# Weight sums of two slots in one operation, in place, and six plain slots instead of seven

## The chip, the cores and the metric

The kernel runs on one core of a Trainium2 chip. The metric is the device time of one execution in microseconds (us). Three runs of the kernel before took 715.67, 717.20 and 717.89 us; the median is 717.2 us. All times below come from those runs or from one profiled execution on the hardware.

## What is computed

For each of four batches of 1024 tokens with 512 features the reference does

```python
scale = cond @ norm_w.T + 1.0
ms = jnp.mean(x * x, axis=-1, keepdims=True)
h = x * (scale[:, None, :] * jax.lax.rsqrt(ms + EPS))
u = h @ up_w.T                       # up_w: 4096 x 512
val, gate = jnp.split(u, 2, axis=-1)
h = val * jax.nn.gelu(gate, approximate=False)
hq = h + jax.lax.stop_gradient(act_quant(h) - h)
wq = down_w + jax.lax.stop_gradient(weight_quant(down_w) - down_w)
y = hq @ wq.T                        # down_w: 512 x 2048
return y + x
```

`act_quant` rounds every row to 8-bit integers by its largest value, `weight_quant` rounds the weights to -1, 0 and 1.

## The kernel before

**Tiling.** The 2048 channels of the hidden layer are 16 slots of 128 (`j` = 0 to 15), each with a value half and a gate half of `up_w`: two 128 x 512 blocks, 512 KB together. A batch's tokens are two halves of 512. A matmul here has a 128 x 128 stationary block and 512 columns, and every f32 operand is split into a high and a low f16 part, so that one product of two blocks takes three f16 matmuls.

**Two kinds of slots.** A plain slot (`plain_half`, lines 803-834, and `plain_first` for slot 0) does value and gate for two token halves straight: 4 results x 12 = 48 matmuls. The other slots (`slot`, lines 858 on) take the value and gate block as a 2 x 2 scheme of seven products in place of eight, each with six matmuls of 512 columns: 42 matmuls. For the seven products the four quarter blocks of a weight slot must first be added and subtracted: `s_sums`, lines 523-529, four operations of 128 x 256 on f32. In the first batch the weights are being built, and slots `j < SEVEN` = 7 are plain, the nine others go by the seven products; in the three later batches all slots do, from what the first batch prepared.

**Steps for a slot's weights** in the first batch: SP loads them (`w_load`) into a buffer of `H` that `W_SLOT` names; their largest value gives a power of two (`w_range`, line 447 a DVE reduction), POOL or ACT multiplies by it (`w_scale`, lines 474-476); `w_rows` splits them into f16 parts (ACT line 499, DVE line 500) in the buffer `H[:, 15 + j % 2]` and issues a transposing transfer (line 501). `s_sums` writes the four combinations to one shared buffer `sf` = `H[:, 17]`. `s_high` (ACT, line 539) and `s_low` (line 543, DVE for odd slots, POOL for even ones) split these; `s_spill` writes the slot to DRAM, with a transposing transfer ahead for slots of the seven products (line 554 and 547). Later batches load it back (`s_load`).

**What sets the order.** All engines' instructions are first recorded by the code (class `Book`), and then emitted in an order that is written out as a packed table `ORDER`. Each engine runs its own queue in that order, with semaphores between the engines. So the program order of the code says what depends on what, and the table says what stands ahead of what on an engine.

**The start.** PE begins with matmuls on zeros (`keep_warm`, line 1185), then transposes the first tokens (line 1169) and the weights of slots 0 and 1 (line 484), whose f16 parts ACT and DVE write out (lines 509 to 521 for weights, 1173 and 1177 for tokens), and starts with slot 0 (line 849). The tokens of the second half (tiles 4 to 7) are scaled by 1/rms on ACT and POOL (lines 1162 and 1164) and transposed a little later.

Of the kernel before, what the change touches and what calls it, by code (L numbers as in the profile page):

```python
# [13 lines left out]
F16 = mybir.dt.float16  # L14
# [9 lines left out]
P = 128  # L24
# [12 lines left out]
PLACE = {4: 0, 5: 1, 6: 2, 2: 3, 3: 4, 0: 5, 1: 6}  # L37
# [35 lines left out]
class Book:  # L73
# [29 lines left out]
    'c-mcB2Y40b5}i#j1V|{UKnOh`AWcA2qzQsb5wU><MHEGv=(8fI=tD(CY@nz#dj~A2s7O&kB%vcBAU&az0MfGa&YAz;oA~zol6&vo',  # L103
    '-M`G7Idf+A#!DsnM^9)C*`bx>u%6Phq`Dl@Ku+s16{#k>HAxcXfTl~nhFS&Jq)T*^l@rQ8kt(tZW9;?c)sX`IORGsaDaP1)HAfEV',
    'Z(3REW41MVj#R)k+jR%t9oNm;1fP#;MOh`aFw#D)D?jN4_$EmL`AgHJBK|)o4{A1MN|ZPWb#&bL;&j=iTQR~(O_iVZLitnAmNU9b',
    '<D{od)C$r<j$v-@W4$()PV$3}kpbEocNJsC19}jjpVBiJbq7|yQw#Mn*`!4nvyaThnS3oL9c8k%kYVzgay7}=MI3fi9u^xUZ`#g_',
    'Gz0TA#5V!fbp$r-CLifVvKVt$k}}vq7Iu0Bdq0G|<>2!lN(&`PBRLDUEwWF;<tx2Zrfa6G*E+Z|Q@+rivJAUujBoSwJ$**H$_Shj',
    '`3@^7(gsqfH6>M+W8Ru_P4H~U`5WSFh&^u8suB-tEWkQn!ajK1CU59KsU=fz)nP3o_2h3|jFtX_I}X5x4ROab{ahv~eKtwjVr4f<',
    '6P&#l?=F^0qzzV(fsu-&hu$q$;4Bd%u+)CNL%xCKI8PRA`K)fl4tirQfnTn{4vu3LPvUivc9!>Wwk@ukti2=~))CpFyRp*sc7Kk1',
    'ua{t#T<<MF#uCldmB2)j+%8kGFCsDrqw>l|*z+K)Bn@krXzTnA_wsmJ9?%~0rS=Qn5Bd41{w^JKr?vvND@rq<HNtQ@P&){#_}0$U',  # L110
    '2X-C_{;_)|N<H8zMHXp$e3~NH!&^P&79EORUo5}l`d8&Hl|aKHtqt6+z?l|7UYIV;v5xMr2uJB83xMWdl&}1&2n1HZtSR_zqcl*i',
    ';CEp6sHR)|?6terNGoMrr2wh*Y@I!2pmxCLclCOF`pcgci=;$&&mAlDT+G-T{#gsZo@3|Q%agW)TGB@U126un^ifq<w!O5I&-8Y9',
    'U4ZqUFyC+5M$SiEFEAfv0v+Fg2g(E0uVTg&87H$eA9!}N(HC{#y-~25$Z<njBlxk0EJbuQm#VTyS7|ex&6fGVYzBDYGrbbH-LG8f',
    '^Lh`ydrt2~RJ4`Ru<mM20spka+PcC=1sJsr)<jlF!@7R8dC!9dGhnkCwuTS&S{qm71HBHPc~v#U#5Vm0c6k;%K82Yd1?~h9w+2!F',
# [12 lines left out]
    '`N0kP4$gFzHQ_nIOdTNgbrU{MN8C4;l^TYhY2Sd^hdUw4sOcQ<Qioh9V*K)ju@FaI0&d@L`R#W@ri=EDng=eb<aUM(5UruE#d0}Z',
    'odJul#{WbptqiH7TZrmY^UgY>%pmQ(u5fV>WfFeQ56cAH)5C~Y&ag=n;7uMIfzcw*W<0h*K?$<cUoi!+0`D4G_9n0Gv)6V&KN0WL',
    '`Dv`>05atVSm_tg2#vvDE{l?tm_z^8TKMCg35ahhx&qUE9N{=n&MZ+8df;yR*7+<2ag*%r=u{!E+O4bww&>e>BSyRk49}7F0eu-B',
    '6O6Zb=nZ!`Pw<ab0{`|P$IJ<@!19ZsB*@$!A=edRuIL~_ocF#$Y*Sem=^lL_t7A5-59@6}G{W*wgQ*h5cf5QjotgKgFIcRMIP5(o',  # L130
    'S85(+`6s3i$miX`r*C1EJQ6LwmV$SYk>pZbmx|RaKwO<4yW<3EizpWp2P5=F8Hg<2-(q1Nl>TDFQCH-_ESVuU+m+K0#R9~<1@%-0',
    'vB=|h=+#kBwhm>qhf_M640n&pW2Pt>8$)z5xIGUZ%rh$$K<l=YXY_vQ4IWr;@myetEKsti$dAyhwZU`Ff=}s#(B=K{_bs%?-?9C_',
    'j~q$0SVl4|KgA<+5Q{bCaUE+&p}z-#VVLioU3g@I^%C*Q6}W@ku}i55oK-l+7-ZX~h8A~@>Z+q$q>Js2_fU;)(s8EsiOn1JZJga~',
    '*vSV6bKN40@C3_4laY}&Tjuys%A0<<2i&m4W)z%Bv6{1nc`+Mn5!fLcx`j2b)0JBh4|_c}({!I<s;y~oSLI%%pWs|Ya96y|AlUhv',
    'R>QD@;&BVCM=ob(ZKHq3Fi{S;?IErbOVT3dMDT|@nC(yLquBdOb$fL7K{cWEf_NyotNoR$p_-{SE{Db>4q1J3ohLoh6A3pU%WO49',
    'As<yUPNClx7I%mnswZ`-uu7#`A~M{H#a2e;OLV%*KH2!<Pg8f?(fRtT<xR2tahq;IMMaGF(CL~MxcZhereYPFQCIW6>%d@{xZB0e',
    'UU2SqWxnOeWbbMc)jI;6BEgGFl`%|TwljA@0iQsmufeDfLko<uv*V!P>tRO$Y(!MwtTRf26|2}{48j;lg&mTly6%c`lvqYz3>*E8',
    'wO6%@;FM--uCRJYK%Q-`D{W20Rx9~jnR$<BCbGEG8dMb`pB0~qyB6O~^=o%p#OeCW5#i0`-$y55ymfX_jI8A97U&Mt$?nLq%vQtf',
    'JqDOBqo*CdphHU6dVfIut_UBHm+TWON~*`_w6i7$vu!n%v7@72tv_BeE4X7NkiE>VA)-%UC9V9Z7h?BUffKhN7Yp)ITiE4YX#2}h',
    'nTXXwEB#K%NUUZr!25T=mS2WFf?P0-$me10pt(>3P1Av>zMqb*d8@tvHWrIx@^N&2Ay&8mZ0?xyb+AWH@PIO=u0XYW7>ewDWMi_;',  # L140
    'WBRBucX>T#9%LTm@es5IH9uJ)#g9r>BtP7Q$e0W4T_>NYtGoE^D5&z0c%7yDeZ;bwz8~MQR^FubOL>h-IqGO_!4=dY(Rb~GMd1kS',
    '`(~)hRr(0@HL`~uM(rV{!N$XfPSO9P>~_%}D}kS{f%#W-s8zj}Ayd2l0KK->bf&A8uLXlO^qrzYSYbUp>5d`LF$JDesa+nijzPp1',
    'B8?@r)D8~X$cOxQ<ShYbzid@;U;Py4Ccu85V(x-4!%#_n-W^s8rs-PbiRc(73&J(v$N!jC?x&Ag)%iB!<^}!JFj!4@%N?j29B*cT',
    'C$nUt)e+B!_XKxB`HQsGb$YWYu^!MSB?oh5GhO9BO_4j1DJtkuDXDsMq3xdmQc`_4U>U~E)hA&0`lyXXt^vD>SFyC`o5%_qG1t;?',
    'Sn!*khMscDkjS5;S8KVzRUn@L^@(yTSSnu`%cJE<oAEWd1Fx^+-S=S^v&(JBbfYa(eS#b^QeH$&Xk8ib^~Zjdw_s=PT`%CGuW7S4',
    '^frsAD}kUSi;kmUC}xcYhGKRivSXI`0H3ZkW^l&<RAp1)9oDq0hXqyRD7jB3m?Btc)jT7cSRQNjm%DGX*7e<nlZcC3EIW(UMekYW',
    '<iY&C7HTfZXJ(fpj~U}RmEts2itqE1wW}E`eI4Y4nO;e;Q$r<R!LHundotU!sn^Er!>|*{Dt|Y)>qsoui>cU%|EZkQe8qFdYpva;',
    'CJv(xt`$>yJAKs<)j6zWb4;(z2yPB*!lG2>3&CGU5E)rQ6qiIbwex;W@ShkN8Mt$u@nK0na6j~E`o9>LkysK9n@!_)g)%%0{H#NC',
    'Ugf{}P|1|_y*A)%)E0keO<ff<3xV`NVzr%L5n`<ncjSA!?6xlaB57~9*sdLepTaa#KO&8S^&$V(hE0O9(jxdhj58~U=WW*mAxpg!',
    '4iD&+BI}`t>hkt8P@H7yWUrr@?|-&>=b*2q#VcE<H{;=(Jl{`^EM5lpRx;l@%&>FA>$f7l`iUE%x>d*Z@Q!PsnrBy_53;HFxaUY`',  # L150
# [1602 lines left out]
```

## Time and profile before

| what | value |
|---|---|
| three runs | 715.67, 717.20, 717.89 us |
| the profiled execution's own time | 716.0 us |
| its span, first to last instruction | 714.2 us |
| granted TensorE clock, mean | 1.000 |
| busy: DVE, ACT, POOL | 527.8, 432.8, 144.2 us |
| read from and written to DRAM | 63.73 and 23.11 MB |

PE is TensorE, DVE VectorE, ACT ScalarE, POOL GpSimd, SP the engine that issues the transfers. A group line gives the source line, the engine, what is written and read (partitions x elements), how often, the busy time and the mean duration in ns, then the idle time just ahead of it and who ended it. A line of windows gives start and end, then the busy time of PE, PE's weight loads, DVE, ACT and POOL with the number of instructions in brackets, the granted clock, the DMA engines' busy share and GB/s. A line of the timeline gives start and duration in us, engine, line and operation. Durations there include the fill of a pipelined engine, so neighbours on PE and DVE overlap by a little.

### The profile page before, as it was taken

What the parts mean: (1) busy time and instruction counts of PE and PEld (TensorE: products, weight loads), DVE (VectorE), ACT (ScalarE), POOL (GpSimd) and SP (SyncE); (2) the same over time, 40 slices, a digit from 0 to 9 for tenths busy, and PEclk for the clock granted to TensorE, in tenths of its full rate; (3) what the DMA queues carried; (4) which work ended last, traced back from release to release, by engine and by line L of the source; (5) the groups of instructions that cost most, each with busy time, mean ns of one, the idle gap of its engine ahead of it and who ended that gap; (6) DMA issues with size and microseconds to landing.
All of it is one profiled execution on the core that took longest, in us unless ns stands there. A gap on an engine that the chain in (4) does not pass through costs nothing.

```text
span 714.2 us, 10170 instructions
## 1 busy us (share of the span) xinstructions
PE 707.6 (99%) x3642; PEld 357.5 (50%) x3642; DVE 527.8 (74%) x837; ACT 432.8 (61%) x739; POOL 144.2 (20%) x161
## 2 busy tenths in 40 slices
PE   8999999999999999999999999999999999999998
PEld 4544444444444446655444455555444444444854
DVE  7968899998478896767659756775638846547895
ACT  5688889886578675654547476453434565334362
POOL 3675521120200005440202032800110000000010
PEclk9999999999999999999999999999999999999999
DMA  8778999999899973777345754566344354433324
GB/s 291 237 223 221 232 230 275 230 190 228 260 212 238 248 238 92 231 165 152 99 133 121 153 142 123 155 171 120 72 137 159 82 132 98 110 118 111 120 87 165
DMA packets 182943, 121.46 MB, mean 170 GB/s; under 512 B 144598, under 2 KB 150503, under 8 KB 182892
## 3 DMA queue, kind: packets, MB, share of 16 engines
q1 hardware_dynamic: 182346, 120.68, 64.8%
q8 instruction: 28, 0.46, 0.2%
q14 instruction: 23, 0.19, 0.1%
q10 hardware_dynamic: 546, 0.13, 0.1%
HBM read 63.73 MB, written 23.11 MB: 122 GB/s over the span
## 4 chain that ended last, share of the span: by engine, by line
PE 98%; DVE 2%; issue 0%
PE A L791 41%; PE E L791 21%; PE B L791 10%; PE po L1077 9%; PE E L806 5%; PE A L806 3%; PE B L806 2%; PE po L1027 2%; PE E L1027 1%; PE B L1077 1%; PE A L1027 1%; PE A L1185 1%; DVE wam L447 0%; PE E L1077 0%; PE A L1077 0%; PE B L1027 0%
## 5 line engine op out<-in xcount | busy, mean ns | idle before, releaser
L791 PEld LDWEIGHTS <-SXY 128*128 128x128 f16 x2226 | 217.7, 98 | 247.7 <-issue 0.2
L791 PE MATMUL A<-R,SXY 128*128 128x512 f16 x1200 | 291.0, 379 | 0.0
L791 PE MATMUL E<-R,SXY 128*128 128x512 f16 x600 | 152.5, 379 | 0.0
L923 ACT ACTIVATE gm<-H 128x512 f32<-128x512 f32 x120 | 75.6, 630 | 56.0 <-DVE R L924 45.3
L924 DVE TENSOR_TENSOR R<-R,gm 128x512 f32<-128x512 f32 x120 | 85.7, 714 | 29.1 <-ACT gm L923 28.5
L868 DVE TENSOR_TENSOR E<-A,v 128x512 f32<-128x512 f32 x57 | 39.7, 697 | 60.6 <-PE A L791 51.6
L791 PE MATMUL B<-R,SXY 128*128 128x512 f16 x318 | 82.7, 379 | 0.0
L1004 DVE TENSOR_TENSOR H<-H,am 128x1024 int8<-128x1024 f32 x64 | 77.0, 1222 | 0.0
L1009 ACT CAST R<-H 128x1024 bf16<-128x1024 int8 x64 | 65.3, 1042 | 18.1 <-DVE H L1004 17.9
L942 POOL PARTITION_ALL_REDUCE am<-R x8 | 15.6, 1950 | 256.8 <-DVE R L924 256.8
L1077 PE MATMUL po<-wd,R 128*128 128x256 fp8e4 x448 | 63.2, 273 | 0.0
L885 ACT ACTIVATE t<-B,sg 128x512 f32<-128x512 f32 x57 | 38.9, 682 | 36.2 <-PE B L791 36.1
L876 ACT COPY B<-A 128x512 f32<-128x512 f32 x57 | 32.8, 576 | 44.5 <-PE A L791 37.8
L1077 PEld LDWEIGHTS <-R 128*128 128x128 bf16 (+1 forms) x512 | 50.1, 98 | 18.7
L888 DVE SCALAR_TENSOR_TENSOR H<-A,sg,t 128x512 f32<-128x512 f32 x57 | 42.5, 746 | 20.7 <-PE A L791 19.8
L904 DVE TENSOR_TENSOR v<-A,v 128x512 f32<-128x512 f32 x57 | 39.1, 686 | 22.1 <-PE A L791 21.8
L901 ACT ACTIVATE t<-E,sg 128x512 f32<-128x512 f32 x57 | 38.7, 681 | 24.4 <-PE E L791 24.4
L907 DVE SCALAR_TENSOR_TENSOR H<-v,sg,t 128x512 f32<-128x512 f32 x57 | 45.2, 794 | 8.1 <-ACT t L901 8.0
L880 ACT COPY v<-E 128x512 f32<-128x512 f32 x57 | 33.2, 582 | 19.9 <-PE E L791 12.8
L806 PEld LDWEIGHTS <-SXY 128*128 128x128 f16 x216 | 21.0, 98 | 24.7 <-issue 0.3
L655 POOL TENSOR_SCALAR ssq<-ssq 128x2 f32<-128x2 f32 x12 | 4.2, 349 | 143.0 <-ACT xt L684 109.2
L1118 DVE SCALAR_TENSOR_TENSOR xr<-po,dq,xr 128x256 f32<-128x256 f32 (+1 forms) x36 | 21.8, 608 | 9.9 <-PE po L1077 4.4
(286 smaller groups left out, 864.1 us busy)
## 6 DMA issues: line engine op xcount, KB each, us to landing
SXY<-s_dram SPq DMA_DIRECT2D x63, 256.0 KB, 3.3
SXY<-s_dram SPq DMA_DIRECT2D x21, 384.0 KB, 3.4
H<-in_L_cond_up_w_dram SPq DMA_DIRECT2D x13, 512.0 KB, 4.8
s_dram<-SXY SPq DMA_DIRECT2D x6, 896.0 KB, 5.7
xr<-in_x_dram SPq DMA_DIRECT2D x19, 256.0 KB, 3.8
out_dram<-xr SPq DMA_DIRECT2D x19, 256.0 KB, 3.2
H<-in_x_dram SPq DMA_DIRECT2D x8, 512.0 KB, 5.1
s_dram<-SXY SPq DMA_DIRECT2D x10, 384.0 KB, 5.1
```

What stands on the lines that cost most here:

```text
L791: PE.matmul(o, s[:, w, k, :], xs(l, k), start=start and n == 0, stop=stop and n == len(TERMS) - 1, skip_group_check=True,)
L806: PE.matmul(ps, a[k // 2][:, w, k % 2, :], XP[:, l, k, h * TOK : (h + 1) * TOK], start=n == 0, stop=n == len(terms) - 1,)
L868: DVE.tensor_tensor(cur["E"], cur["A"], cur["v"], ALU.add)
L885: ACT.activation(cur["t1"], pb, AF.Gelu, scale=gain(g, 1))
L888: DVE.scalar_tensor_tensor(h_half(g - 1, 0), prev["A"], gain(g - 1, 0), prev["t1"], ALU.mult, ALU.mult)
L904: DVE.tensor_tensor(cur["v"], cur["A"], cur["v"], ALU.add)
L907: DVE.scalar_tensor_tensor(h_half(g - 1, 1), prev["v"], gain(g - 1, 0), prev["t2"], ALU.mult, ALU.mult)
L923: ACT.activation(gm, v, AF.Abs)
L924: DVE.tensor_tensor(m, m, gm, ALU.max)
L1004: DVE.tensor_tensor(whole(v), v, r.to_broadcast([P, 2, TOK]), ALU.mult)
L1009: ACT.copy(q, by_tile(whole(v)))
L1077: PE.matmul(po, w[:, j], m, start=start and j == 0, stop=stop and j == n - 1, skip_group_check=True,)
```

## The change

Five things are changed in the code. The four sums of a slot are now made for two slots at once: the operations are 128 x 2 x 256, and `s_sums` is called for even `j` only. They are written back over the slot's own weight blocks, so `sf` becomes a view of the slot's weight buffer, and `W_SLOT` puts slots `j` and `j + 1` of a pair side by side. Because the weights are overwritten, the f16 rows for the transposing transfer are split off earlier, by a function of its own (`w_cast`), in `H[:, 16 + j % 2]`. `SEVEN` is 6, so slot 6 goes by the seven products. Two buffers are moved (`FT`, the junk output of `first_sum(0)`), and the table `ORDER` is replaced as a whole.

```diff
-PLACE = {4: 0, 5: 1, 6: 2, 2: 3, 3: 4, 0: 5, 1: 6}
+PLACE = {6: 0, 4: 1, 5: 2, 2: 3, 3: 4, 0: 5, 1: 6}
...
 ORDER = (
-    '5*6$@hON`O)6`g^sV=9S)9n`y1+l00@~>`h$?-py<lOQ',
...
-    W_SLOT = [14, 12, 13, 8, 9, 10, 14, 12, 13] + 3 * [14, 12, 13]
+    W_SLOT = [14, 15, 12, 13, 8, 9, 10, 11] + 2 * [12, 13, 14, 15]
...
-    sf = H[:, 17].rearrange("p t (n f) -> p (t n) f", n=2)
+    def sf(j):
+        return wn(j).rearrange("p t (n f) -> p (t n) f", n=2)
...
-    SEVEN = 7
+    SEVEN = 6
...
+    cast = set()
+
+    def w_cast(j):
+
+        cast.add(j)
+        n = H[:, 16 + j % 2].bitcast(F16).rearrange("p t (n w f) -> p (t n) w f", n=2, w=2)
+        a = 0 if j < SEVEN else 1
+        ACT.copy(n[:, a:, 0], sf(j)[:, a:])
+        DVE.tensor_tensor(n[:, a:, 1], sf(j)[:, a:], n[:, a:, 0], ALU.subtract)
+
     def w_rows(j):
 
-        v = H[:, 15 + j % 2].bitcast(F16).rearrange("p t d -> p (t d)")
-        n = v.rearrange("p (n w f) -> p n w f", n=4, w=2)
-        f = wn(j).rearrange("p t (n f) -> p (t n) f", n=2)
+        if j not in cast:
+            w_cast(j)
+        v = H[:, 16 + j % 2].bitcast(F16).rearrange("p t d -> p (t d)")
         a = 0 if j < SEVEN else 1
-        ACT.copy(n[:, a:, 0], f[:, a:])
-        DVE.tensor_tensor(n[:, a:, 1], f[:, a:], n[:, a:, 0], ALU.subtract)
...
     def s_sums(j):
-        v = wn(j).rearrange("p t (n f) -> p t n f", n=2)
-        a11, a12, a21, a22 = v[:, 1, 0], v[:, 1, 1], v[:, 0, 0], v[:, 0, 1]
-        (POOL if j < 4 else DVE).tensor_tensor(sf[:, 0], a21, a22, ALU.add)
-        (POOL if j < 4 else DVE).tensor_tensor(sf[:, 2], a11, a21, ALU.subtract)
-        (POOL if j < 6 else DVE).tensor_tensor(sf[:, 1], sf[:, 0], a11, ALU.subtract)
-        (POOL if j < 6 else DVE).tensor_tensor(sf[:, 3], a12, sf[:, 1], ALU.subtract)
+
+        c = W_SLOT[j]
+        v = H[:, c : c + 2].rearrange("p s t (n f) -> p s t n f", n=2)
+        a11, a12, a21, a22 = v[:, :, 1, 0], v[:, :, 1, 1], v[:, :, 0, 0], v[:, :, 0, 1]
+        eng = POOL if j < 4 else DVE
+        eng.tensor_tensor(a22, a21, a22, ALU.add)
+        eng.tensor_tensor(a21, a11, a21, ALU.subtract)
+        eng.tensor_tensor(a11, a22, a11, ALU.subtract)
+        eng.tensor_tensor(a12, a12, a11, ALU.subtract)
...
-    FT.append(H[:, 11])
+    FT.append(H[:, 7])
...
         if n == 0:
-            j = wn(0)[:, 0]
+            j = H[:, 0, 0]
...
-        if n < NJ:
-            s_sums(n)
...
-        if n < NJ:
-            s_all(n)
         if j + 3 < NJ:
             w_scale(j + 3)
             if j < SEVEN:
                 w_rows(j + 3)
+            elif j % 2 == 0:
+                w_cast(j + 3)
+        if j % 2 == 0 and n < NJ:
+            s_sums(n)
+        if n < NJ:
+            s_all(n)
```

The new table moves instructions on every engine. Three places follow. The source lines of the kernel after are some 8 to 11 higher from line 500 on.

The first is DVE at the start, just ahead of PE's first matmul of slot 0. `E_103` and `po_102` are PSUM buffers that hold transposed weights and tokens; line 509 (517 after) writes weights, line 518 (526 after) their low part, line 1177 (1188 after) the low part of tokens, line 1145 (1156 after) sums a token tile's squares. Before:

```order
L447 TENSOR_REDUCE wam_99<-H 128x2
L454 TENSOR_SCALAR sw<-wam_104 128x2
L321 TENSOR_SCALAR wam_99<-wam_99 128x2
L457 RECIPROCAL iv_106<-sw 128x2
L454 TENSOR_SCALAR sw<-wam_99 128x2
L509 CAST SXY<-E_103 128x2x256
L457 RECIPROCAL iv_105<-sw 128x2
L518 TENSOR_TENSOR SXY<-E_103,SXY 128x2x256
L1177 SCALAR_TENSOR_TENSOR R<-po_101,scT,R 128x512
```

The same place on DVE after the change:

```order
L447 TENSOR_REDUCE wam_99<-H 128x2
L320 TENSOR_SCALAR wam_104<-wam_104 128x2
L320 TENSOR_SCALAR wam_99<-wam_99 128x2
L454 TENSOR_SCALAR sw<-wam_104 128x2
L454 TENSOR_SCALAR sw<-wam_99 128x2
L457 RECIPROCAL iv_106<-sw 128x2
L457 RECIPROCAL iv_105<-sw 128x2
L1156 SCALAR_TENSOR_TENSOR R,ssq_0_88<-H 128x512
L1188 SCALAR_TENSOR_TENSOR R<-po_102,scT,R 128x512
L517 CAST SXY<-E_103 128x2x256
```

The sum of squares and a low part of tokens have moved ahead of the first cast of weights; the low part of weights, which stood directly behind the cast, comes later.

The second is PE at the same time: its step into slot 0. `E_98`, `A_91`, `po_102` are PSUM buffers, the rows of line 1185 (1196 after) the matmuls on zeros. Before:

```order
L484 MATMUL E_98<-ident,H 128x128
L1169 MATMUL po_102<-ident,H 128x128 x2
L1169 MATMUL A_91<-ident,H 128x128
L1185 LDWEIGHTS H
L1185 MATMUL A_94<-H 128x512
L849 LDWEIGHTS SXY
L849 MATMUL B_92<-R,SXY 128x512
```

After the change PE has this order there (line 860 is line 849 of before):

```order
L1196 MATMUL A_94<-H 128x512
L484 MATMUL E_103<-ident,H 128x128
L484 MATMUL po_102<-ident,H 128x128
L860 LDWEIGHTS SXY
L860 MATMUL A_94<-R,SXY 128x512
L484 MATMUL po_102<-ident,H 128x128
L1180 MATMUL A_91<-ident,H 128x128
L484 MATMUL po_102<-ident,H 128x128 x2
```

Slot 0 now begins with its value half (buffer `A_94`) rather than its gate half (`B_92`), and behind transposes of slot 1's weights into `po_102`, the buffer that DVE's line 1188 reads before.

The third is POOL from slot 0's sums on: lines 526 to 529 are the four sums, 476 scales weights, 656 (667 after) computes 1/rms of token tiles 4 to 7, and 1164 (1175 after) scales tiles 5 and 7 by it. Before:

```order
L529 TENSOR_TENSOR H<-H 128x256
L656 TENSOR_TENSOR rs_0_89<-ssq_0_88,neghalf 128x4
L543 TENSOR_TENSOR SXY<-H,SXY 128x3x256
L1164 TENSOR_SCALAR H<-H,rs_0_89 128x512 x2
L526 TENSOR_TENSOR H<-H 128x256
```

The same stretch on POOL after, from the first sum of slots 0 and 1 (line 537) on:

```order
L537 TENSOR_TENSOR H<-H 128x2x256
L476 TENSOR_SCALAR H<-H,iv_106 128x512
L667 TENSOR_TENSOR rs_0_89<-ssq_0_88,neghalf 128x4
L538 TENSOR_TENSOR H<-H 128x2x256
L1175 TENSOR_SCALAR H<-H,rs_0_89 128x512
L454 TENSOR_SCALAR sw<-wam_99 128x2
L539 TENSOR_TENSOR H<-H 128x2x256
L476 TENSOR_SCALAR H<-H,iv_100 128x512 x2
L1175 TENSOR_SCALAR H<-H,rs_0_89 128x512
```

Tile 7's scaling, which stood directly behind tile 5's, now has a sum of two slots and two weight scalings ahead of it; slot 0's low part (line 543), which stood ahead of both, has gone behind.

170 lines of the change are left out of this document (84 added, 86 removed).

## The prediction

> **What bounds the kernel now.** I read first the page's line of busy times and the chain of work that ended last.
>
> ```profile
> PE 707.6 (99%) x3642; PEld 357.5 (50%) x3642; DVE 527.8 (74%) x837; ACT 432.8 (61%) x739; POOL 144.2 (20%) x161
> PE 98%; DVE 2%; issue 0%
> ```
>
> PE is busy for 99% of the span and is 98% of the chain. A busy PE need not be at its pitch, so next the timeline of PE in the first batch, at products of six matmuls of 512 columns:
>
> ```profile
> 163.59 1.46 PE L791 MATMUL A<-R,SXY 128*128 128x512 f16 x6
> 164.88 1.46 PE L791 MATMUL A<-wd,R 128*128 128x512 f16 x6
> 166.18 1.46 PE L791 MATMUL E<-wd,SXY 128*128 128x512 f16 x6
> ```
>
> Starts are 1.295 us apart for six, so one costs 0.216 us. Then the windows of the first batch, where the changed work lies (PE, PE's weight loads, DVE, ACT, POOL, then clock, DMA share, GB/s):
>
> ```profile
> 0.00:20.00 20.00, 16.76 (x85) 9.33 (x86) 16.00 (x71) 11.17 (x22) 7.31 (x14) 1.00 0.89 299
> 20.00:40.00 20.00, 20.00 (x103) 10.24 (x101) 17.26 (x32) 14.01 (x29) 15.51 (x21) 1.00 0.74 226
> 80.00:100.00 20.00, 20.00 (x95) 9.06 (x93) 19.89 (x35) 17.91 (x33) 4.83 (x5) 1.00 0.93 251
> 140.00:160.00 20.00, 20.00 (x95) 9.08 (x93) 18.63 (x32) 16.29 (x30) 5.34 (x7) 1.00 1.12 219
> ```
>
> All PE idleness that an order could remove lies before 20 us; behind it PE is full. DVE is full from 80 to 100 us (19.89 of 20) and yet makes PE wait nowhere. So the time can fall in two ways only, fewer matmuls or an earlier start, and rise wherever a moved instruction now comes later than PE wants it.
>
> **The change, part by part.**
>
> *Six plain slots.* Slot 6 in the first batch goes from 48 matmuls to 42. Six times 0.216 is **-1.30 us**, in full, since PE is full there and nothing else can swallow it unless something becomes late.
>
> *The start.* These rows are of DVE and PE just ahead of slot 0:
>
> ```profile
> 13.45 1.22 DVE L447 TENSOR_REDUCE wam<-H 128x2 f32<-128x1024 f32 x1
> ...
> 15.13 0.68 DVE L509 CAST SXY<-E 128x512 f16<-128x512 f32 x1
> ...
> 16.45 2.06 DVE L1177 SCALAR_TENSOR_TENSOR R<-po,scT,R 128x512 f16<-128x512 f32 x3
> ```
>
> ```profile
> 15.87 1.76 PE L849 MATMUL B<-R,SXY 128*128 128x512 f16 x6 [0.23 <-DVE SXY L509]
> ```
>
> Before, the cast that releases slot 0's first matmul comes directly behind the last reduction and its small followers, and PE starts slot 0 at 15.87. After, a sum of squares of 512 elements (0.68, as the rows of that size below) and a low part (2.06 for three, 0.69 each) stand between. The reduction ends near 14.67, the six small operations bring 15.1, the sum of squares 15.8, the low part near 16.5; PE transposes slot 1's weights into the buffer that this low part frees, and its next row is the first matmul of slot 0: about 16.65, **0.8 later**. Behind that it waits less, because tokens' low parts and transposes that stood between the matmuls of slot 0 are then already done. Following both orders by hand to where the first 36 matmuls of f16 and the last transposes ahead of tile 4 are through, before is at 25.05 and after at about 25.5. I take **+0.5 us**, with the ends -1.0 and +1.0: the low end is what PE still loses around these starts if the new order hides it (0.23 in the row above and some short ones), the high end the 0.8 with nothing made good. The clock was granted at 1.00 in the window; I cost the different spread of the matmuls on zeros at nothing.
>
> *Sums.* Their price on DVE before, and that of operations of 512 elements per partition, each from the groups by shape in the first 205 us:
>
> ```profile
> L526 DVE TENSOR_TENSOR H<-H 128x256 f32<-128x256 f32 x12 | 6.0, 496 | 1.6 <-POOL SXY L543 1.1 <-ACT H L474 0.5
> L527 DVE TENSOR_TENSOR H<-H 128x256 f32<-128x256 f32 x12 | 4.9, 411 | 0.0
> L528 DVE TENSOR_TENSOR H<-H 128x256 f32<-128x256 f32 x10 | 4.1, 415 | 0.1
> L529 DVE TENSOR_TENSOR H<-H 128x256 f32<-128x256 f32 x10 | 4.1, 414 | 0.0
> ```
>
> ```profile
> L924 DVE TENSOR_TENSOR R<-R,gm 128x512 f32<-128x512 f32 x31 | 21.2, 683 | 3.8 <-ACT gm L923 3.7
> L907 DVE SCALAR_TENSOR_TENSOR H<-v,sg,t 128x512 f32<-128x512 f32 x11 | 9.5, 860 | 1.1 <-ACT t L901 1.1
> L834 DVE SCALAR_TENSOR_TENSOR H<-E,sg,t 128x512 f32<-128x512 f32 x13 | 9.4, 738 | 2.5 <-PE E L806 2.5
> ...
> L868 DVE TENSOR_TENSOR E<-A,v 128x512 f32<-128x512 f32 x12 | 8.3, 694 | 6.8 <-PE A L791 6.8
> L904 DVE TENSOR_TENSOR v<-A,v 128x512 f32<-128x512 f32 x12 | 8.2, 684 | 1.2 <-PE A L791 1.0
> L888 DVE SCALAR_TENSOR_TENSOR H<-A,sg,t 128x512 f32<-128x512 f32 x11 | 8.2, 744 | 3.5 <-PE A L791 3.5
> ```
>
> 44 single sums go (6.0 + 4.9 + 4.1 + 4.1 = 19.1 us), 24 paired ones come. The trace has no operation on 2 x 256 in place; the nearest row is L924 (512 elements, f32, written over an input): 24 x 0.683 = 16.4. The other end is two singles each, 2 x 19.1 / 44 = 0.87, so 20.8. I take 0.683, as the same number of elements and also in place: -2.7 us of DVE. Slot 6 takes away two of L834 (1.5) and adds one each of L868, L888, L904 and L907 (2.98): +1.5. DVE is relieved by about 1.2 us net in the first batch, none of it on the path, so it is worth **0**. Six matmul results of slot 6 that ACT now copies are hidden as those of slots 7 to 15 are.
>
> On POOL 20 single sums become 8 paired ones:
>
> ```profile
> L529 POOL TENSOR_TENSOR H<-H 128x256 f32<-128x256 f32 x6 | 5.7, 950 | 0.2
> ...
> L527 POOL TENSOR_TENSOR H<-H 128x256 f32<-128x256 f32 x4 | 2.9, 728 | 0.1
> ```
>
> ```profile
> L694 POOL TENSOR_TENSOR H<-H,sc 128x512 f32<-128x512 f32 x8 | 11.9, 1487 | 4.6 <-ACT H L692 4.6
> ```
>
> A pair costs between 2 x 0.728 = 1.46 and 2 x 0.950 = 1.90; the row of 512 elements (1.49) lies near the low end, and I take 1.45. Why single sums spread is seen at two rows that start together, one on each engine:
>
> ```profile
> 45.65 1.45 POOL L529 TENSOR_TENSOR H<-H 128x256 f32<-128x256 f32 x1
> ```
>
> ```profile
> 45.57 0.96 DVE L543 TENSOR_TENSOR SXY<-H,SXY 128x768 f16<-128x768 f32 x1 [0.83 <-ACT SXY L539]
> ```
>
> POOL's sum took 1.45 instead of 0.73: about DVE's remaining time longer. So a sum on POOL that meets a DVE operation of two SBUF inputs stands still for it; one meeting costs up to that operation's length, here 0.7. [...]
>
> *Where POOL's sums are on the path.* Tiles 5 and 7 of the second token half are scaled on POOL before PE transposes them:
>
> ```profile
> 24.03 1.36 POOL L1164 TENSOR_SCALAR H<-H,rs 128x512 f32<-128x512 f32 x2
> ```
>
> ```profile
> 25.05 0.60 PE L1169 MATMUL po<-ident,H 128*128 128x128 f32 x4
> ...
> 27.43 0.38 PE L1169 MATMUL A<-ident,H 128*128 128x128 f32 x2
> ```
>
> Both are scaled by 25.39 before, two microseconds ahead of need. After, one sum and two weight scalings stand between them. Adding POOL's rows from 1/rms on (near 20.2) with 1.45 for a pair brings tile 7 to about 27.25, and PE's first transpose of it falls at about 27.4. So **0**, with 0.15 us of cover; at 1.90 for each of the pairs ahead it is 1.2 us late.
>
> *Rows and late slots.* In-place sums force the split into f16 rows to come ahead of the sums. The case with the least room is slot 15, whose low part is DVE's and whose sums must be transposed by DMA before PE's fifth product (the 166.18 row above):
>
> ```profile
> 154.72 1.21 DVE L543 TENSOR_TENSOR R<-H,R 128x1024 f16<-128x1024 f32 x1
> ```
>
> ```profile
> 156.01 2.89 SPq L554 DMA_TRANSPOSE SXY<-R  x1
> ```
>
> ```profile
> SXY<-R SPq DMA_TRANSPOSE x1, 4.3
> ```
>
> The transfer lands at 156.01 + 4.3 = 160.3, 5.9 us ahead. Adding up DVE's queue in both orders with the durations by shape puts 136.0 us of work ahead of that low part before and 140.2 after: 4.2 later, though DVE has less in all, because other work (sums over tokens, maxima) is now ahead of it. PE asks 0.8 earlier (1.30 - 0.5). 5.9 - 4.2 - 0.8 leaves 0.9 us: **0**, thinly. DVE's idle time would absorb part of any more.
>
> *The rest.* In later batches slot 6's weights come back by other transfers; PE waits for no load there, so 0. The moved buffers and the junk row change waits of SP and ACT in the first 10 us, where DVE (16.00 of 20 us busy) is the one that PE follows: 0, and if DVE stops being that cover it is inside the ends of the start.
>
> **Sum.** -1.30 + 0.5 = -0.8. The profiled execution's own time is 716.0 us (span 714.2 and 1.8 around it), so it would be 715.2; it lies 1.2 below the median of the runs, 717.2. Against that median: **716.4 us**.
>
> **The rivals.**
> (a) *The start loses nothing.* For it: the matmuls that follow are less interleaved with waits. Against: 0.8 us is added ahead of the first one in DVE's own queue. -1.30 alone gives 715.9; with the full -1.0 of the start, 714.9. Chance 0.17.
> (b) *Tile 7 comes late.* For it: 0.15 us of cover, and the pair of rows at 45.6, where a sum doubled. Against: in that stretch most of DVE's inputs are in PSUM. At 1.90 a pair, +1.2: 717.6, no difference from before. Chance 0.18.
> (c) *Paired sums on DVE cost two singles, and late slots wait* (slower). From 0.87 instead of 0.683, 24 x 0.187 = 4.5 us later at slot 15, less 0.9 of room: PE waits 3.6, so 716.4 + 3.6 = 720.0. It decides from 0.683 + 0.9 / 24 = 0.72 us a pair. For it: no row shows this form, and DVE is full from 80 to 100 us. Against: every DVE row here goes by elements, 0.41 for 256 and 0.68 for 512. Chance 0.15.
> (d) *The six matmuls bring nothing*, because slot 6, now in need of transposed sums by the end of plain slot 5, waits as long as it saves: 717.2 + 0.5 = 717.7. Against: its low part can be had well ahead, as slot 7's was. Chance 0.05.
>
> My forecast has 0.45. Chances that a measurement can tell apart (0.3%, or 2.15 us): faster means under 715.05, which takes most of the start's -1.0 beside the -1.30: 0.11. Slower means over 719.35: case (c) and a sum of small delays, 0.18. The same: 0.71. The range leaves out the lower end of (a) and the upper part of (c): 714.8 to 719.6.
>
> **What the profile after would show.** One product of slot 6 at 1.295 us like the others and 3636 matmuls. DVE groups of 128x2x256 at 683 ns (right) or near 870 (case c); POOL's near 1450 or 1900 (case b). PE's first matmul of slot 0 near 16.65. In PE's waits, any row on DVE, POOL or DMA behind 20 us means a step is wrong: for POOL's line 1175 case (b), for line 554's transfer case (c). The prediction fails if PE's start moves by over a microsecond or if such a row exceeds one.

## The result and the profile after

The kernel after takes 720.18 us (median of six runs, 719.57 to 722.30), the kernel before 717.1 in the same comparison. The ratio is 1.0051, with a 95% interval of 1.0033 to 1.0068: slower by 2.4 to 4.9 us. The forecast was 716.4 and its range ended at 719.6.

The profile of after is of an execution of 720.42 us with a span of 718.3. First the page's line of busy times and its chain, to be read beside those of before:

```profile
PE 708.8 (99%) x3636; PEld 358.7 (50%) x3636; DVE 526.6 (73%) x819; ACT 435.0 (61%) x740; POOL 137.1 (19%) x148
PE 92%; DMA 3%; DVE 1%; ACT 1%; SPq 1%; issue 0%; POOL 0%
```

There are six matmuls fewer, 3636, and yet PE is busy 1.2 us longer. DVE and POOL have less to do, as expected. DMA, which had no share of the chain before, has 3%. Next what PE waited for (microseconds in all, times, longest):

```profile
PE E L363 <- DMA H<-in_cond_dram: 1.5, 1, 1.5
PE A L802 <- DVE H L899: 1.4, 1, 1.4
PE A L1196 <- DVE H L269: 1.2, 1, 1.2
PE A L376 <- DVE eps L1133: 0.7, 1, 0.7
PE E L802 <- DVE E L879: 0.3, 1, 0.3
PE E L802 <- DMA SXY<-s_dram: 0.3, 1, 0.3
PE A L860 <- ACT R L1184: 0.3, 1, 0.3
```

The kernel before has two waits of over 0.3 us, at the places of the third and fourth row:

```profile
PE A L1185 <- DVE H L268: 1.2, 1, 1.2
PE A L377 <- DVE mx L370: 1.1, 1, 1.1
```

So the first two rows of after are new, and the largest. Neither names a sum of weights. To see when the time is lost, I counted the matmuls of both profiles back from the last one and compared their starts:

| same number of matmuls left | start before, us | start after | after minus before |
|---|---|---|---|
| 3480 | 34.78 | 35.25 | +0.47 |
| 3240 | 86.53 | 86.93 | +0.40 |
| 2760 | 190.13 | 191.21 | +1.08 |
| 2640 | 215.74 | 218.79 | +3.05 |
| 2460 | 254.59 | 258.10 | +3.51 |
| 0 | 710.64 | 714.38 | +3.74 |

Ahead of slot 6 the kernel before has six matmuls (1.30 us) more to go for the same work, so at equal work after is 0.47 + 1.30 = 1.77 us late at 35 us. The account of this execution is thus: start +1.77, matmuls -1.30, waits around slots 6 and 7 and behind them +0.6, one stretch from 203 to 216 us +1.97, a load at 246 us +0.46, small things +0.2. It compares two single executions: the one of before, at 716.0 us, lies 1.1 below the median of its runs, the one of after near its own, so the account adds up to more than the 3.1 us between the medians.

**The start.** Windows of two microseconds (PE, weight loads, DVE, ACT, POOL, then the granted clock, DMA share, GB/s), first two of before, then those of after and PE's timeline:

```profile
12.00:14.00 2.00, 1.82 (x15) 1.43 (x16) 2.00 (x6) 0.00 (x0) 1.86 (x3) 1.00 1.03 367
14.00:16.00 2.00, 1.77 (x16) 1.36 (x14) 2.00 (x8) 1.91 (x4) 1.63 (x4) 1.00 1.04 398
```

```profile
8.00:10.00 2.00, 1.50 (x8) 0.63 (x6) 1.38 (x5) 1.54 (x5) 0.00 (x0) 1.00 0.86 288
10.00:12.00 2.00, 0.98 (x7) 0.81 (x8) 1.84 (x14) 1.63 (x4) 0.69 (x1) 1.00 1.05 406
12.00:14.00 2.00, 2.00 (x15) 1.92 (x15) 2.00 (x6) 1.76 (x3) 1.36 (x2) 0.70 1.05 390
14.00:16.00 2.00, 2.00 (x11) 2.00 (x10) 2.00 (x10) 0.69 (x1) 0.51 (x1) 0.50 0.72 265
16.00:18.00 2.00, 1.74 (x12) 1.16 (x11) 0.99 (x2) 1.87 (x5) 1.21 (x2) 0.94 0.01 2
```

```profile
9.17 0.33 PE L356 MATMUL po<-ident,R 128*128 128x128 f32 x1
11.02 0.35 PE L363 MATMUL E<-H,R 128*128 128x3 f32 x2 [1.52 <-DMA H<-in_cond_dram]
...
12.65 1.74 PE L1180 MATMUL po<-ident,H 128*128 128x128 f32 x8
14.18 0.42 PE L484 MATMUL E<-ident,H 128*128 128x128 f32 x1
14.39 0.42 PE L1180 MATMUL A<-ident,H 128*128 128x128 f32 x1
...
18.00 0.38 PE L860 MATMUL A<-R,SXY 128*128 128x512 f16 x1 [0.26 <-ACT R L1184]
```

PE stands still from 9.5 to 11.0 for the conditioning rows of the later batches, and is thinly busy around it. Then the granted clock falls to 0.50, from 12.81 to 16.23 us by the trace's record of the clock: transposes start 0.21 us apart, where they did so 0.11 apart before. Slot 0 starts at 18.00 instead of 15.87. The rows come late because ACT issues their load at 3.52 instead of 2.29, behind an activation that waits for a constant which DVE's new order writes later, and behind more weight loads:

```profile
3.51 0.20 ACT L1136 ACTIVATE start_t<-one 128x1 f32<-128x1 f32 x1 [0.94 <-DVE one L251]
3.52 0.41 ACTq L1207 DMA_DIRECT2D H<-in_cond_dram  x1
```

The same 1.5 KB in the profile before, and then after:

```profile
H<-in_cond_dram ACTq DMA_DIRECT2D x1, 1.5 KB, 6.6
H<-in_cond_dram ACTq DMA_DIRECT2D x1, 1.5 KB, 7.4
```

They took 7.4 us, against 6.6 before. In these profiles, the later they were issued, the longer they took: 5.1 to 5.9 us from 1.28 (runs 1, 4, 5, 10 and 12 below), 6.2 to 7.3 from 2.29 (before, runs 6 and 11), 7.0 to 8.6 from 3.5 (after, runs 2, 3, 7 and 8). SP had issued one weight load of 256 KB ahead of them in before (at 2.27) and three in after (at 2.27, 2.78 and 3.28); that these are what held the rows was not shown, as no run moves those loads alone.

**The stretch from 203 to 216 us.** At the end of the first batch each token's scale goes through DRAM and comes back to all partitions (lines 974 to 981; 963 to 970 before). SP's rows, after and then before:

```profile
191.02 0.53 SPq L613 DMA_DIRECT2D xn<-in_L_cond_down_w_dram  x1
191.60 0.42 SPq L613 DMA_DIRECT2D nx<-in_L_cond_down_w_dram  x1
192.93 0.33 SPq L980 DMA_DIRECT2D am_dram<-rows  x1
198.77 0.33 SPq L981 DMA_DIRECT2D am<-am_dram  x1
```

```profile
191.15 0.57 SPq L547 DMA_DIRECT2D s_dram<-R  x1
192.71 0.32 SPq L969 DMA_DIRECT2D am_dram<-rows  x1
195.76 0.33 SPq L970 DMA_DIRECT2D am<-am_dram  x1
...
196.66 0.38 SPq L602 DMA_DIRECT2D nx<-in_L_cond_down_w_dram  x1
```

The row of 4 KB is issued at the same time in both, but after it has two loads of 512 KB directly ahead and takes 5.8 us instead of 3.0. The store of 896 KB (line 547) that before issues 1.6 us ahead of the row does not hold it. DVE's rounding by these scales starts at 202.99 rather than 200.17, PE's wait follows:

```profile
202.99 2.36 DVE L1015 TENSOR_TENSOR H<-H,am 128x1024 int8<-128x1024 f32 x2 [0.36 <-DMA am<-am_dram]
```

```profile
211.88 1.67 PE L802 MATMUL A<-R,SXY 128*128 128x512 f16 x7 [1.37 <-DVE H L899]
```

**The sums.** The groups by shape of after (of DVE's four rows, all of 685 to 689 ns, the first and the last):

```profile
L540 DVE TENSOR_TENSOR H<-H 128x512 f32<-128x512 f32 x6 | 4.1, 689 | 0.1
...
L537 DVE TENSOR_TENSOR H<-H 128x512 f32<-128x512 f32 x6 | 4.1, 685 | 0.1
```

```profile
L538 POOL TENSOR_TENSOR H<-H 128x512 f32<-128x512 f32 x2 | 3.3, 1664 | 0.0
L539 POOL TENSOR_TENSOR H<-H 128x512 f32<-128x512 f32 x2 | 2.7, 1368 | 0.2
L537 POOL TENSOR_TENSOR H<-H 128x512 f32<-128x512 f32 x2 | 2.5, 1271 | 1.8 <-PE po L484 1.8
L540 POOL TENSOR_TENSOR H<-H 128x512 f32<-128x512 f32 x2 | 2.5, 1270 | 0.1
```

A pair costs DVE 0.687 us and POOL 1.27 undisturbed. Slot 15's transposed sums, issued at 160.15 and landing 4.4 later, are there 2.6 us before their product at 167.16.

### The profile page after: what moved, and what is told of

It is laid out like the page before. It is cut to its first block, busy times and chain, and to the rows that moved or that the text cites. A ratio compares the mean times of both kernels' runs of the same rounds, so it can differ in the third digit from the quotient of the medians.

```text
span 718.3 us, 10070 instructions
## 1 busy us (share of the span) xinstructions
PE 708.8 (99%) x3636; PEld 358.7 (50%) x3636; DVE 526.6 (73%) x819; ACT 435.0 (61%) x740; POOL 137.1 (19%) x148
## 4 chain that ended last, share of the span: by engine, by line
PE 92%; DMA 3%; DVE 1%; ACT 1%; SPq 1%; issue 0%; POOL 0%
PE A L802 40%; PE E L802 20%; PE B L802 10%; PE po L1088 9%; PE E L817 3%; PE A L817 2%; PE po L1038 2%; PE B L817 1%; DMA H<-in_cond_dram 1%; PE E L1038 1%; DMA SXY<-s_dram 1%; PE B L1088 1%; PE A L1038 1%; DMA H<-in_L_cond_up_w_dram 1%; DMA s_dram<-R 1%; PE po L1180 1%
## 5 line engine op out<-in xcount | busy, mean ns | idle before, releaser
L802 PEld LDWEIGHTS <-SXY 128*128 128x128 f16 x2268 | 221.9, 98 | 254.7 <-issue 3.1
L802 PE MATMUL A<-R,SXY 128*128 128x512 f16 x1212 | 294.2, 379 | 1.4 <-DVE H L899 1.4
L802 PE MATMUL E<-R,SXY 128*128 128x512 f16 x606 | 157.4, 379 | 0.6 <-DVE E L879 0.3
L1020 ACT CAST R<-H 128x1024 bf16<-128x1024 int8 x64 | 65.6, 1043 | 12.8 <-DVE H L1015 9.5
L802 PEld LDWEIGHTS <-R 128*128 128x128 f16 x168 | 16.4, 98 | 19.9
```

The lines of the kernel that those rows point to most:

```text
L802: PE.matmul(o, s[:, w, k, :], xs(l, k), start=start and n == 0, stop=stop and n == len(TERMS) - 1, skip_group_check=True,)
L1020: ACT.copy(q, by_tile(whole(v)))
```

## The experiments

All of them but two are the kernel after with a few instructions moved in the order, added or split; the arithmetic is left whole. Ratios are to the kernel before in the same comparison.

| run | median, us | ratio and interval | mean clock of its executions |
|---|---|---|---|
| a1_cond_first | 720.31 | 1.0049 (1.0037-1.0061) | 0.995-0.999 |
| a2_busy_wait | 718.28 | 1.0012 (1.0003-1.0021) | 0.999-1.000 |
| a3_loads_before | 720.26 | 1.0046 (1.0033-1.0059) | 0.994-0.998 |
| a4_both | 719.43 | 1.0029 (1.0018-1.0041) | 0.995-1.000 |
| a5_start | 720.22 | 1.0038 (1.0026-1.0050) | 0.998-0.999 |
| b2_no_zeros | 718.83 | 1.0020 (1.0011-1.0030) | 0.993-0.998 |
| d1_six_more | 719.84 | 1.0037 (1.0025-1.0049) | 1.000 |
| c1_single_sums | 718.74 | 1.0026 (1.0015-1.0036) | 0.999-1.000 |
| a7_busy_loads | 717.16 | 1.0001 (0.9992-1.0010) | 0.999-1.000 |
| a8_best | 716.88 | 1.0001 (0.9992-1.0010) | 0.999-1.000 |
| b1_load_ahead | 717.03 | 1.0008 (0.9998-1.0017) | 0.995-1.000 |
| a9_low_part_first | 717.24 | 1.0002 (0.9993-1.0011) | 0.999-1.000 |

**1. The conditioning rows early.** ACT:

```diff
 L1134 DMA H<-in_cond_dram 1x128
+L1207 DMA H<-in_cond_dram 128x3x1
 L1136 ACTIVATE start_t_86<-one 128x1
-L1207 DMA H<-in_cond_dram 128x3x1
```

> The kernel after, with one move in the order: ACT issues the load of the later batches' conditioning rows (line 1207) ahead of its first activation, near 1.2 us instead of 3.52. Theory (the small load queues behind the weight loads that were issued before it, PE waits 1.5 us for it, and the TensorE clock then falls to 0.5): the load lands before PE asks near 9.3, the wait of line 363 is gone, the clock is 1.00 throughout the start, the first matmul of slot 0 comes near 16.7 instead of 18.0, and the time falls by about 1.3 us, to 718.9. Rival (the start is set by DVE's order alone): the wait goes but slot 0 still starts near 18, time 720.2.

The rows landed at 6.4 us, and the time stayed. PE's wait had a next cause:

```profile
PE E L363 <- ACT R L357: 0.7, 1, 0.7
```

PE was idle at about the same place, the clock fell to 0.50 all the same, and slot 0 started at 18.89. My theory of a single late load was wrong; the idle stretch has several causes. (In this execution the clock also rose late: matmuls on zeros start 0.42 us apart up to 9.9 us, where in after the clock rises at 6.0.)

**2. PE kept busy there.** PE, eight matmuls on zeros ahead of line 363:

```diff
 L356 MATMUL po_97<-ident,R 128x128
+L1196 MATMUL A_94<-H 128x512 x8
 L363 MATMUL E_98<-H,R 128x3
```

> The kernel after, with eight more matmuls on zeros on PE directly ahead of line 363, so that PE is busy while it waits for the conditioning rows; no load is moved. Theory (what costs is the clock that falls behind the idle stretch, not the wait itself): the rows land near 10.9 as before, the clock stays at 1.00, the transposes of 12.7 to 16.3 run at 0.107 us instead of 0.214, slot 0 starts near 16.8 and the time falls by about 1.2 us, to 719.0. Rival (the wait of 1.5 us is what costs): no change, 720.2, or up to 0.3 more for the added matmuls.

The wait stayed (1.0 us are left ahead of line 363), the clock did not fall, and the time fell by 1.9 us. Its windows beside those above:

```profile
12.00:14.00 2.00, 1.76 (x16) 1.61 (x17) 1.79 (x6) 1.71 (x3) 1.36 (x2) 1.00 1.03 358
14.00:16.00 2.00, 2.00 (x20) 1.98 (x19) 2.00 (x8) 0.97 (x3) 0.27 (x1) 1.00 0.72 252
```

Twenty matmuls and transposes instead of eleven between 14 and 16 us. In this one profile the row of scales was also quicker (4.65 us): at 35 us it is 0.06 late, where after is 0.47, and the stretch from 203 to 216 us costs it 0.65 where it costs after 1.97. So its 1.9 us need not be the clock's alone.

**3. The loads away from the row of scales.** SP:

```diff
+L613 DMA xn_114<-in_L_cond_down_w_dram
+L613 DMA nx_124<-in_L_cond_down_w_dram
 L579 DMA_TRANSPOSE SXY<-s_dram
-L613 DMA xn_114<-in_L_cond_down_w_dram
-L613 DMA nx_124<-in_L_cond_down_w_dram
 L980 DMA am_dram<-rows
```

> The kernel after, with one move in SP's order: the two loads of down_w (512 KB each, line 613, at 191.0 and 191.6 us) go ahead of the transposing load at 189.5, so that they are no longer issued directly ahead of the row of scales (line 980 at 192.9). Theory (the row and with it the scales of all tokens come back 2.8 us late because 1 MB is queued ahead of it, and DVE's rounding, ACT's cast and then PE follow): the row lands about 3 to 4 us after its issue instead of 5.8, the waits of PE near 207 and 210 us (0.5 and 1.5) go, and the time falls by 1.5 to 2.0 us, to 718.5. Rival (the wait there comes from DVE's and ACT's new order): the row lands earlier and PE waits as before, 720.2.

The row took 3.4 us, as expected, and PE's wait fell to 0.5. Part of this is handed back: the row was issued later, since the small load of line 975 ahead of it now took 5.7 us instead of 4.4.

```profile
194.58 0.33 SPq L980 DMA_DIRECT2D am_dram<-rows  x1
197.98 0.33 SPq L981 DMA_DIRECT2D am<-am_dram  x1
```

```profile
PE A L802 <- DVE H L899: 0.5, 1, 0.5
```

But the median did not move: the executions of this run lost more to the clock. Its five times go with their mean clock: 718.97 at 0.998, 719.84 at 0.997, 720.26 and 720.65 at 0.995, 721.39 at 0.994. By the lost share of the span (0.004 x 718 = 2.9 us between the ends) 2.4 us are lost: most of it reaches the end.

**4. Both moves.** 

> The kernel after with both moves, the conditioning load early and the two loads of down_w ahead. Theory: the two losses are apart and add, 720.2 - 1.3 - 1.8 = 717.1, equal to the kernel before; what is left of the 1.30 us of matmuls saved is eaten by the start's order (about 0.5) and by waits of about 0.5 each near 88-94 and at 246 us. Rival (one wait hides behind the other, or PE is held by something else next): 718.5 or more.

It came out below run 1 by 0.9 us in the medians and 1.4 in the ratios, not 1.8, and its executions still had clocks of 0.995 to 1.000.

**5. The start's order mended, nothing added.** Besides the move of run 1, PE's fourth transpose of line 356 goes behind the third, and ACT's line 357 ahead of its second sum of squares. 

> The kernel after with the start's order mended and no work added: the conditioning rows are loaded ahead of ACT's first activation, PE's fourth transpose of norm_w (line 356) goes directly behind the third, and ACT's copy of it (line 357) ahead of ACT's second sum of squares. Theory (any idle stretch of PE near 9 to 11 us, whoever causes it, lets the TensorE clock fall, and that costs some 2 us; with the conditioning load alone moved, ACT's copy took over as the cause): line 363 starts near 9.3, the clock stays at 1.00 and the time falls by 2 to 3 us, to 717.2 to 718.2, no worse than with the eight added matmuls (718.3). Rival (the clock falls at the start whatever the order after the change): 720.2.

A miss: the wait of line 363 was gone, and PE stood still one instruction further on.

```profile
PE po L1180 <- POOL H L1175: 0.9, 1, 0.9
```

The rival held: in this order DVE, ACT and POOL have the first tokens ready only near 12 us, and with this freed before that, PE still stood idle and the clock fell to 0.50.

**6. The same on the kernel before**, leaving out seven matmuls on zeros:

```diff
 L393 MATMUL B_92<-dg_96,one 128x1
-L1185 MATMUL A_94<-H 128x512 x7
 L364 MATMUL E_98<-H,R 128x3
```

> The kernel before, leaving out the seven matmuls on zeros that PE runs from 8.96 to 10.48 us; nothing else is changed, and the work of the reference is whole. Theory (an idle PE there lets the clock fall): the granted clock falls to 0.5 for some us behind 12 us, mean 0.998, and the time rises by 1.5 to 2.5 us, to 719.2; runs spread more. Rival (the zeros are only filling): no change, 717.3, clock 1.000.

```profile
PE B L343 <- DMA H<-in_cond_dram: 0.9, 1, 0.9
```

```profile
12.00:14.00 2.00, 1.98 (x11) 1.98 (x12) 1.93 (x7) 0.81 (x2) 1.43 (x3) 0.50 1.03 346
14.00:16.00 2.00, 2.00 (x10) 1.54 (x9) 2.00 (x6) 0.00 (x0) 1.89 (x3) 0.50 1.02 377
```

It is slower by 1.4 us with no other change. None of its nine executions has a mean clock above 0.998, where eleven of the 21 of the kernel before in the same comparison have 1.000. But its profile does not show what began the fall: the clock was at 0.50 from 7.9 us on, ahead of the place of the seven matmuls at 9 us, in an execution in which PE had waited 0.9 us for a first small load (line 343). It shows a longer low stretch, to 18.1 us, and slot 0 at 18.78; and it shows that nothing of such a loss is made good, with 3.00 us at 35 us and 3.04 at the end. Three executions with a mean clock of 0.998 took 717.87 to 718.30, six with 0.993 took 718.65 to 719.35.

**7. Slot 6 with 48 matmuls again** (its first matmul six times more, on top of run 2). 

> The kernel after with the eight matmuls on zeros of the run a2_busy_wait, and the first matmul of slot 6 issued six times more (it writes the same result again), so that slot 6 costs PE 48 matmuls again. Theory (six matmuls are worth 6 x 0.216 = 1.30 us in full): 718.3 + 1.3 = 719.6. Rival (the six matmuls saved were hidden, since slot 6 waits for other things, 0.3 to 0.5 us of it seen at 88 us): 718.3 to 718.9.

Its ratio is 0.0025 above run 2's, 1.8 us, with about 1.1 to either side by the two intervals. That fits 1.30 and excludes zero. The six matmuls were worth their time.

**8. Single sums.** On top of run 2, each paired sum as two, in place and at the same place of the order:

```diff
-L537 TENSOR_TENSOR H<-H 128x2x256
+L537 TENSOR_TENSOR H<-H 128x256 x2
```

> The kernel after with the eight matmuls on zeros, and every sum of two slots issued as two operations of 128 x 256, one for each slot, at the same place of the order and still in place. Theory (sums are off the path; the paired form saves DVE 24 x 0.14 = 3.4 us and POOL little, and PE does not see it): within 0.5 us of 718.3. Rival (late slots have no room, as the prediction's third rival has it): waits of PE at slots 6 to 15, up to 2.5 us more, 720.8.

Its profile has one wait of PE at slots 6 to 15, 0.13 us, where run 2 has 0.15. The median is 0.5 above run 2 and the ratios differ by 0.0014 with wide spread (716.61 to 720.52); the profile puts its largest wait behind the start, 1.5 us, ahead of 210.4 us, where no sum is made. So the form of the sums is not what slowed the kernel; whether it is worth half a microsecond stays open.

**9. Busy PE and moved loads together.** 

> The kernel after with the eight matmuls on zeros and the two loads of down_w moved ahead as in a3_loads_before. With the clock held at 1.00, the spread that hid the second loss should be gone. Theory (the row of scales comes back late behind 1 MB of loads: it took 4.65 to 5.82 us in the six profiles with the loads directly ahead and 3.38 in the two with the loads moved): the row takes 3.4 us, PE's wait near 207 to 211 falls from 0.6-2.0 us to 0.3-0.7, and the time from 718.3 to 717.3-717.8. Rival (DVE's and ACT's new order sets that wait): 718.3.

717.16, and level with the kernel before. One of eleven executions took 1943.93 us for a reason not found, and the profile fell on it, so only the times are used (the median of the other ten is 717.06). Against run 3, which differs by the eight matmuls alone, it is 3.1 us faster; against run 2, which differs by the loads alone, 0.8 by the ratios, which their intervals do not tell from none.

**10. All three.** 

> The kernel after with all three: conditioning rows loaded early, eight matmuls on zeros where PE is idle near 9 to 11 us, loads of down_w moved ahead. Theory (the early rows end PE's wait ahead of line 363 a little sooner, the zeros keep the clock): 717.0, between the kernel before and 0.5 us below it; the matmuls saved (1.30) are then met by about 1 us that DVE's and ACT's order costs at the start. Rival (start set by DVE and ACT only): as a7_busy_loads.

716.88, and no worse or better than the kernel before, nor than run 9, which lacks the early rows alone. Counted back from the last matmul as in the table above, its profile is 0.56 us ahead of before at 35 us, 0.18 at 190 and 0.03 behind at the end. No wait around 207 is left; what PE still waits for at the start:

```profile
16.95 0.38 PE L860 MATMUL A<-R,SXY 128*128 128x512 f16 x1
```

```profile
PE po L484 <- DVE R L1188: 0.4, 1, 0.4
```

**11. The late row on the kernel before**: SP's load at 196.7 moved ahead of line 969. 

> The kernel before, with one load of down_w (512 KB, line 602, issued at 196.7 us) moved to directly ahead of the row of scales (line 969 at 192.7). Theory: the row takes 4 to 5 us instead of 3.04, DVE's rounding (line 1004) starts 1 to 2 us later than 200.2, and a wait of PE appears near 205 to 210 us, 0.3 to 1.5 us: 717.3 to 718.6. Rival (before's order has room there, so a late row alone makes no wait): 717.1.

```profile
191.92 0.38 SPq L602 DMA_DIRECT2D nx<-in_L_cond_down_w_dram  x1
193.10 0.43 SPq L969 DMA_DIRECT2D am_dram<-rows  x1
198.87 0.32 SPq L970 DMA_DIRECT2D am<-am_dram  x1
```

```profile
206.81 1.46 PE L791 MATMUL E<-R,SXY 128*128 128x512 f16 x6 [0.33 <-DVE E L868]
```

The row took 5.8 us behind a single load, rounding began at 202.65, and PE lost 0.48 us at 206 and nothing elsewhere. That a load ahead delays the row, and the row PE, is shown; the time (1.0008, interval from 0.9998) cannot be told from none. In this profile, with before's order on DVE and ACT, much the same lateness costs a quarter of the 1.97 us that it costs in after.

**12. One DVE instruction of the start moved back**, on top of run 10: line 1188 ahead of line 1156. 

> The mended kernel a8_best with one more move: on DVE the first low part of tokens (line 1188, into the buffer that PE's transposes of slot 1 wait for) goes ahead of the sum of squares (line 1156) that the new order put in front of it. Theory (the prediction's term for the start: slot 0 starts later because of what stands ahead in DVE's queue; in a8_best PE waits 0.6 us for that low part at 16.1): slot 0 starts 0.4 to 0.6 us sooner than 16.95 and the time falls to 716.4, 0.4 us below the kernel before. Rival (ACT's casts, which end near 16.7, set the start as well): at most 0.2 us, 716.7.

No gain. PE's wait for line 1188 was gone and one for ACT's casts (0.3 us) was in its place; the rival held. Slot 0 started at 17.45, not sooner than 16.95 but later: in this execution PE had also waited 0.4 us for ACT's line 357 and 0.3 for a tile scaled on POOL.

## Why the prediction was wrong

*The six matmuls* (-1.30 us) were right: they are gone from the profile, and run 7 puts them back.

*The sums* were right. DVE's pair was taken at 0.683 us and took 0.687; POOL's was taken at 1.45 and took 1.27, or up to 2.06 in the one that raised its group's mean to 1.66. That one started at 35.86, beside a DVE operation with both inputs in SBUF (line 554, 35.84 to 36.78); in before single sums that met such operations took 1.59 at 40.48 (line 771) and 1.32 at 56.83 (line 543), one beside DVE's line 834, which reads PSUM, 0.73 at 42.14. Tile 7 was ready at 28.6 us instead of 27.25, since from 1/rms on POOL took 7.6 us where I had 7.05; PE's first transpose of it starts at 28.76 and did not wait, being late itself. Run 10 is as close (27.59 and 27.73), so this step held with 0.1 us to spare, and in part by luck. Slot 15 had 2.6 us of room where I had 0.9, in run 10 too. The rivals on POOL, on DVE's price and on a wasted saving did not come about.

*The start* is the step that failed. The prediction took +0.5, from DVE's queue, and said of the rest: "I cost the different spread of the matmuls on zeros at nothing", and of moved waits of SP and ACT in the first 10 us: "0, and if DVE stops being that cover it is inside the ends of the start". With the idle stretch filled and the loads in place (run 10) the term is -0.56 + 1.30 = +0.74 and slot 0 starts at 16.95, against 16.65 in the prediction. There DVE's queue was the right account, and only a little short: PE waits 0.4 us for just the low part that the prediction named, as in run 8 (slot 0 at 16.86, the term 0.89). In the other profiles with the eight matmuls the term is larger, 1.36 to 1.55 (runs 2, 7 and 12), and run 12 shows that ACT's casts hold PE about as long.

In the kernel after itself, 1.77 us were lost in the profiled execution, because the order moved matmuls on zeros away from the stretch where PE waits. Every pair of runs that differs by the eight matmuls alone has the loss, in the medians 1.9 us (after and run 2), 3.1 (3 and 9) and 2.5 (4 and 10), by the ratios 2.8, 3.2 and 2.0, each clear of none by their intervals. The records of the clock agree: all five profiles of the new order without the eight matmuls (after, runs 1, 3, 4 and 5) have a stretch of 3.41 us at half clock, and none of the five readable ones with them has one (runs 2, 7, 8, 10 and 12). In runs 3 and 4 together, executions with a mean clock of 0.998 took 717.7 and 719.0 us, those with 0.994 to 0.996 took 719.6 to 721.4; one with 1.000 took 718.46 and does not fit, so the clock is not all of it. The small load that moved behind big ones made no difference that the times show (run 1 against after, run 10 against 9). The prediction's own test, "the prediction fails if PE's start moves by over a microsecond", named the start.

What brings the clock down was not shown. In after it stood at 0.50, with transposes at twice their pitch, from 12.81 to 16.23, 3.41 us; in run 6 for three times that. PE was not simply idle ahead of it: in the 3.41 us before the fall it was busy for 1.89, and never stood still for longer than 1.5. Nor does the clock rise at one time: in all profiles but run 9's the first seven matmuls start within 0.01 us of the same times, and yet the first recorded rise of the clock lies anywhere from 3.9 to 10.0 us; executions of one kernel differ as well (0.994 to 0.998 in run 3). The prediction had rows that bear on this, the zeros in both orders and a clock of 1.00 with them in place, and didn't ask what holds that clock up. Its reading of 1.00 for the whole start was wrong, too: before's first matmuls on zeros start 0.43 us apart, twice 0.216, and the record of the clock begins only at 5.5 us, ahead of which the column says nothing.

*The rest* failed too: "PE waits for no load there, so 0". That was said of slot 6's weights, and there was no term for what the new table does to other transfers. The table that was replaced also orders SP's transfers at the end of the first batch, and I compared orders at three places, none of them SP's. Two loads that moved ahead of a 4 KB row cost 2.0 us in the profile. The same stretch costs 1.6 to 1.9 us in four more profiles with the loads there (runs 1, 5, 7 and 8), 0.65 in run 2, and 0 to 0.66 in the four with the loads moved (runs 3, 4, 10 and 12). In the times moving them is worth 1.4 us by the ratios of run 4 against 1, 0.8 of run 9 against 2, which is not clear of none, and nothing visible in run 3, where the mean clock fell furthest (0.994). A late load of a slot's weights (0.46 at 246 us) and the 0.6 around slots 6 and 7 were not tried.

Taken together: the saving of 1.30 us is real, 0.7 of it or more is eaten by the order at the start even where the clock holds, and the rest of the loss came with the new order, not with the new sums. With two edits of that order, the eight matmuls and the moved loads, the kernel equals the one before (1.0001, 0.9992 to 1.0010), and the third, the early rows, adds nothing that shows; no version that beats it was found.

What stays open: executions of the kernel before have a mean clock of 0.995 to 0.997 as well (ten of 21 in the comparison with run 6), and those with 0.997 are no slower than those with 1.000 (716.18 to 717.17 against 716.05 to 718.03), though the two with 0.995 are among the slowest (717.95 and 718.12). So it seems to matter where the low stretch lies, but no profile of such an execution was taken. Profiles of the new order point the same way: with the stretch at 12.8 to 16.8 us the start costs 1.77 to 2.67 us at equal work (after, runs 1 and 5; in the last two the clock also rose late), with it at 10.8 to 14.3 only 1.24 to 1.42 (runs 3 and 4), no more than run 2 loses without one.

## What to carry to other kernels

Where a change replaces an order, compare every queue, that of the transfers first: look at each small transfer on a chain (a row of scales, a handful of conditioning values) and look for loads issued shortly ahead of it (run 11: one load of 512 KB 1.2 us ahead, and the row took 5.8 us instead of 3.0). Filler matmuls at a start are not idle decoration (eight of them were worth 1.9 to 3.1 us in the medians here): find the stretches in which PE waits or is thinly busy, see whether the filler still lies in them, and price a fallen clock at the work that follows at half speed (in after 3.41 us of it, with transposes 0.21 us apart instead of 0.11).

## What the runs showed of the hardware that was not expected

Freeing one cause of an idle stretch did nothing, three times over (runs 1 and 5: 720.31 and 720.22 us against 720.18; run 12: 717.24 against 716.88): the next engine's wait filled it, and the clock fell to 0.50 in the first two. The cheapest remedy was to add work (eight matmuls on zeros, 1.9 us in run 2). The 4 KB row of scales took 4.6 to 5.8 us in the seven readable profiles in which one or two loads of 512 KB were issued up to 2.2 us ahead of it, and 3.0 to 4.2 in the six others; a store of 896 KB 1.6 us ahead left it at 3.0 in the kernel before. A sum of two slots on POOL cost 1.27 us where two single ones cost 1.46, so about 0.19 us is saved, more than on DVE (0.687 against 2 x 0.414, 0.14).
